# State-space layer: one batch's step-size exponentials moved ahead of the next decays in two of eight steps

## The chip, the cores and the metric

The kernel runs on one core of a Trainium2 chip. The metric is the device time of one execution in microseconds (us); the engines are TensorE (PE in the profile, with its weight loads as PEld), VectorE (DVE), ScalarE (ACT), GpSimd (POOL) and SyncE (SP), each with its own queue that it works through in order.

## The reference

A decoder of four blocks; each block has three layers (attention or a substitute, cross attention, a feed-forward part), and behind each the input is added and normalised. There are 4 sequences (batches) of 512 positions with 128 features. The change lies in the first layer of the second block, `L1_attn`, which is a state-space layer:

```python
xz = x @ W_in                                   # 128 -> 2 x 256
xi, z = jnp.split(xz, 2, axis=-1)
xc = silu(causal_conv4(xi, conv_w) + conv_b)    # 256 channels
dt, Bm, Cm = jnp.split(xc @ W_x, [8, 24], axis=-1)   # 8, 16 and 16 wide
delta = jax.nn.softplus(dt @ W_dt + b_dt)       # step sizes, 256 channels
A = -jnp.exp(A_log)                             # 256 x 16
dA = jnp.exp(delta[..., None] * A)              # decays
dBu = delta[..., None] * Bm[:, :, None, :] * xc[..., None]
h_t = dA_t * h_{t-1} + dBu_t                    # 16 states a channel
y_t = sum over states of h_t * C_t
y = y + xc * D
return y * silu(z) @ W_out
x = layernorm(x + that)
```

## The kernel before

All twelve layers run one after the other on the core, the tail of one interleaved with the start of the next. Every engine executes its instructions in the order in which the Python program emits them (`manual_schedule` for all five), so the order of the calls is the order of the queues; semaphores between engines follow from which instruction reads or writes which tile.

In `l1_attn` time runs along the free axis (512 positions) and the 256 channels are two halves `c` of 128 partitions. The 16 states are taken two at a time (`NQ = 2`), so a batch has `steps = 8` steps, and the loop over `g` runs through 4 x 8 = 32 steps plus one; `b` is the batch of a step and `j` its number in the batch. One step has these parts:

- `decays(g)`: four Exp activations on ScalarE (L2160), each of 511 elements, into `das[g % 2]`. They are issued one step ahead of their use.
- `spread(g, "B", c)` and `spread(g, "C", c)`: TensorE spreads one row of B or C over all partitions with a selecting weight (L2146 into two PSUM tiles `pb`, L2152 into a single PSUM buffer `pc`); ScalarE copies C to SBUF (`cs`, L2153). These too are one step ahead.
- `recurred(g)`: VectorE multiplies B with `du` (L2171) for both halves, then scans along time with the decays (L2174); GpSimd multiplies the states with C (L2178).
- `summed(g - 1, c)`: TensorE adds the states of the step before into PSUM (L2187), with an identity as weight.

Into this loop the next batch is prepared, by two agendas that run a piece at its step. `prepare(b + 1)` is called at `j == 1`. The agenda `early` then does at steps 1 to 6: the two halves of the convolution, `selected` (the product with `W_x`), `exponentials(0)`, `exponentials(1)`, and the gates. The agenda `late` does `logarithm(0)` at step 4 and `logarithm(1)` at step 5, and `third` (`ends`) at step 6 finishes the step sizes on GpSimd.

The softplus is formed as max(v, 0) + log(1 + exp(-|v|)), the logarithm by a polynomial in product form. `exponentials(c)` (L2097 to L2114) is one matmul into the PSUM tile `pdt` (L2100) and seven activations on ScalarE: Abs (L2105), Relu (L2106), two Exp (L2107, L2108) and three Squares (L2111). `logarithm(c)` (L2116 to L2122) is five VectorE instructions over `pdt`, the Squares `sq` and the exponential `ab`. `pdt`, the gates' `psz` and the products `px` and `pscv` share one PSUM buffer, and `sq` has one buffer for both halves, so `exponentials(1)` can start only when `logarithm(0)` is through. Before the loop, the first batch is prepared beside the previous layer, and the last batch has no successor to prepare, so `exponentials` runs in the loop in three batches.

In the kernel before, `early.run(g)` is called once a step, after the decays of the next step and after the first half of the sum, and ahead of the spreading:

Of the kernel before, what the change touches and what calls it, by code (L numbers as in the profile page):

```python
# [186 lines left out]
def decoder_kernel(ctx: ExitStack, tc: tile.TileContext, x, ctxT, mask1, mask3, packs, offsets, out, layers):  # L187
# [1844 lines left out]
    def l1_attn(w, cur, new, last, room):  # L2032
# [23 lines left out]
        early, late = Agenda(), Agenda()  # L2056
# [80 lines left out]
        def spread(g, kind, c):  # L2137

            b, j = divmod(g, steps)
            m = made[b]  # L2140
            if kind == "B":
                pb = psum2("pb")
                m["B", j, c] = pb
                for i in range(NQ):
                    n = j * NQ + i
                    nc.tensor.matmul(pb[:, i, :], lhsT=pick[:, n : n + 1].to_broadcast([P, P]), rhs=m["bc"], start=True, stop=True)  # L2146
                return
            if c == 0:
                m["C", j] = work[0].tile([P, NQ, S], F32, tag="cs", name="cs")
            pc = psum_v("pc", "a0")  # L2150
            n = NS + j * NQ + c
            nc.tensor.matmul(pc, lhsT=pick[:, n : n + 1].to_broadcast([P, P]), rhs=m["bc"], start=True, stop=True)  # L2152
            nc.scalar.copy(m["C", j][:, c, :], pc)  # L2153

        def decays(g):
            b, j = divmod(g, steps)
            for c in range(2):
                for i in range(NQ):
                    n = j * NQ + i
                    nc.scalar.activation(  # L2160
                        das[g % 2][:, c, i, 1:], made[b]["de"][:, c, 1:], AF.Exp, scale=nav[:, c, n : n + 1]
                    )

        def recurred(g):

            b, j = divmod(g, steps)
            m = made[b]
            m["h", j] = [work[0].tile([P, NQ, S], F32, tag=f"hh{c}", name=f"hh{c}") for c in range(2)]
            pbs = [m.pop(("B", j, c)) for c in range(2)]
            for c in range(2):  # L2170
                nc.vector.tensor_tensor(pbs[c], m["du"][:, c, None, :].to_broadcast([P, NQ, S]), pbs[c], ALU.mult)  # L2171
            for c in range(2):
                flat = m["h", j][c].rearrange("p n t -> p (n t)")
                nc.vector.tensor_tensor_scan(  # L2174
                    flat, das[g % 2][:, c].rearrange("p n t -> p (n t)"), pbs[c].rearrange("p n t -> p (n t)"),
                    0.0, ALU.mult, ALU.add,
                )
                nc.gpsimd.tensor_tensor(m["h", j][c], m["h", j][c], m["C", j], ALU.mult)  # L2178

        def summed(g, c):  # L2180
            b, j = divmod(g, steps)
            m = made[b]
            if j == 0 and c == 0:
                m["acc"] = [psum_v("acc", at) for at in "vy"]
            for i in range(NQ):
                n = j * NQ + i
                nc.tensor.matmul(  # L2187
                    m["acc"][c], lhsT=ident, rhs=m["h", j][c][:, i, :], start=(n == 0), stop=(n == NS - 1),
                    skip_group_check=True,
                )  # L2190

        def outputs(b):
            m = made.pop(b)
            yt = keep.tile([P, 2, S], F32, tag="yt", name="yt")
            for c in range(2):
                nc.vector.scalar_tensor_tensor(  # L2196
                    yt[:, c, :], m["xc"][:, c, :], w["dd"][:, c : c + 1], m["acc"][c], ALU.mult, ALU.add
                )
            nc.gpsimd.tensor_tensor(yt, yt, m["sz"], ALU.mult)
            ys = keep.tile([P, NT, D], F32, tag="ys", name="ys")  # L2200
            yps = []

            def projected():
                yp = psum_a("yps")
                yps.append(yp)
                for t in range(NT):
                    for c in range(2):
                        nc.tensor.matmul(
                            yp[:, t * P : (t + 1) * P], lhsT=yt[:, c, t * P : (t + 1) * P], rhs=wout[:, c, :],
                            start=(c == 0), stop=(c == 1),  # L2210
                        )

            def summed_up():
                nc.vector.tensor_tensor(
                    ys, yps[0].rearrange("p (t d) -> p t d", t=NT), state_x[:, b * NT : (b + 1) * NT, :], ALU.add
                )

            stats, norm, turn_over = finish_pieces(b, ys, new, last, split=True)
            return projected, summed_up, stats, norm, turn_over
# [29 lines left out]
        for g in range(total + 1):  # L2249
            b, j = divmod(g, steps)  # L2250
            if j == 1 and b + 1 < B:
                first, second, third = prepare(b + 1)
                early.add(g, first)
                late.add(g + 3, second)
            if j == 6 and b + 1 < B:
                third()
            if g < total:
                recurred(g)
            if g + 1 < total:
                decays(g + 1)  # L2260
            for c in range(2):
                if 0 <= g - 1 < total:
                    summed(g - 1, c)
                if c == 0:
                    early.run(g)
                if g + 1 < total:
                    spread(g + 1, "B", c)
                    spread(g + 1, "C", c)
            if j == 0 and b >= 1:
                late.run(g)  # L2270
                pieces = outputs(b - 1)
                if b < B:
                    early.add(g + 7, pieces[:1])
                    late.add(g + 7, [lambda two=pieces[1:3]: [f() for f in two]])
                    late.add(g + 8, [lambda end=pieces[3:]: [f() for f in end]])
            late.run(g)
            new["room"] = room_ahead if j % 2 and b == B - 1 else None
            yield PIECE
# [7 lines left out]

    run = dict(
        L0_attn=l0_attn, L0_xattn=l0_xattn, L0_ffn=l0_ffn, L1_attn=l1_attn, L1_xattn=l1_xattn, L1_ffn=l1_ffn,
        L2_attn=l2_attn, L2_xattn=l2_xattn, L2_ffn=l2_ffn, L3_attn=l3_attn, L3_xattn=l3_xattn, L3_ffn=l3_ffn,
    )  # L2290
# [156 lines left out]
```

## Time and profile before

| | us |
|---|---|
| median of 3 runs | 2677.82 (2677.05 to 2679.14) |
| profiled execution | 2676.14 |
| its span, first to last instruction | 2674.3 |
| state-space layer, first to last multiply-and-scan step | about 545 to 820 of the span |
| busy over the whole span: PE, DVE, ACT, POOL | 2413.6, 1708.0, 1244.2, 1056.5 |

One execution is profiled; times in the profile count from its first instruction. In a group's line the first part is line, engine, operation, and output<-inputs, then the shapes and how often; after the first bar busy time in us and the mean of one in ns; after the second the idle time of the engine just before these instructions, and what ended most of it. In a timeline a line has its start, its length, and in square brackets the idle time before it with what released it. A matmul in 32-bit floats shows as two records (two passes). In a table of stretches the columns are the length and the busy time of PE, PEld, DVE, ACT and POOL, each with its number of instructions, then TensorE's granted clock as a part of full speed, the DMA share and GB/s. In the waits the columns are who waited for whom, us in total, how often, and the longest.

### The profile page before, as it was taken

The numbers are of one execution on the slowest core, as the hardware profiler recorded it, in microseconds if no ns is written. First come the engines' busy times: TensorE is split into PE (matmuls) and PEld (weight loads), VectorE is DVE, ScalarE is ACT, GpSimd is POOL, SyncE is SP. The second block draws the span as 40 slices with busy tenths as digits, with TensorE's granted clock in tenths as the row PEclk, the third lists the DMA queues.
The fourth block names the chain that finished last, engine by engine and source line by source line (L and its number), as shares of the span: only waits on it lengthen the run. The fifth ranks groups of instructions, "written<-read, shape, count | busy, mean of one in ns | idle before, by whom it ended". The sixth has DMA issues, their size and how long they took to land.

```text
span 2674.3 us, 37907 instructions
## 1 busy us (share of the span) xinstructions
PE 2413.6 (90%) x14198; PEld 1171.3 (44%) x14218; DVE 1708.0 (64%) x3092; ACT 1244.2 (47%) x2517; POOL 1056.5 (40%) x1376
## 2 busy tenths in 40 slices
PE   5998889978877989999999999997988899899998
PEld 1333334433334444444444555554455333445665
DVE  6896951289997665555555555565855888564444
ACT  3775432377652434333233555453543678343221
POOL 2342520157675327555542444443345242320000
PEclk9998999989988999999999999998998899999999
DMA  5421310000002400000000000002102231310000
GB/s 154 120 80 58 102 36 0 0 0 0 0 16 76 149 7 1 0 1 1 0 1 1 15 1 13 13 6 80 51 1 60 67 99 41 129 45 5 13 11 14
DMA packets 76712, 97.98 MB, mean 37 GB/s; under 512 B 24048, under 2 KB 62704, under 8 KB 76528
## 3 DMA queue, kind: packets, MB, share of 16 engines
q1 hardware_dynamic: 75376, 93.72, 12.2%
q8 instruction: 112, 1.84, 0.3%
q10 hardware_dynamic: 1152, 1.84, 0.2%
q14 instruction: 72, 0.59, 0.1%
HBM read 63.92 MB, written 33.49 MB: 36 GB/s over the span
## 4 chain that ended last, share of the span: by engine, by line
PE 65%; DVE 14%; ACT 8%; POOL 5%; issue 4%; DMA 2%; SPq 1%; POOLq 0%; DVEq 0%; ACTq 0%
PE av L721 4%; PE psgu L1962 4%; PE psve L1312 4%; PE scc L1149 4%; PE avc L1222 3%; PE yT L1355 3%; PE ype L1978 3%; PE ptc L1209 3%; PE psh L1647 3%; ACT pr L1183 3%; PE sc L682 2%; DVE top L979 2%; PE avx L1007 2%; PE psqk L1494 2%; PE st L698 2%
## 5 line engine op out<-in xcount | busy, mean ns | idle before, releaser
L1193 POOL TENSOR_TENSOR pr<-pr,zs 128x1024 f32<-128x1024 f32 x192 | 237.4, 1254 | 236.2 <-DVE zs L1190 207.3
L686 DVE TENSOR_REDUCE top<-sc 128x2 f32<-128x1024 f32 x256 | 300.8, 1216 | 44.8 <-PE sc L682 42.1
L707 ACT ACTIVATE pT<-st 128x512 f32<-128x512 f32 x512 | 276.2, 597 | 88.6 <-PE st L698 85.3
L1183 ACT ACTIVATE pr<-scc,nm 128x256 f32<-128x256 f32 (+3 forms) x384 | 198.5, 527 | 177.7 <-DVE nm L1171 99.1
L979 DVE TENSOR_REDUCE top<-scx 128x4 f32<-128x616 f32 x256 | 192.1, 794 | 88.1 <-PE scx L966 76.9
L985 ACT ACTIVATE pTx<-stx 128x512 f32<-128x512 f32 x256 | 139.2, 596 | 204.3 <-PE scx L966 145.6
L2178 POOL TENSOR_TENSOR hh<-hh,cs 128x1024 f32<-128x1024 f32 x64 | 149.3, 2355 | 74.5 <-DVE hh L2174 50.8
L1171 DVE TENSOR_REDUCE nm<-scc 128x2 f32<-128x1024 f32 (+3 forms) x128 | 102.4, 821 | 118.5 <-PE scc L1156 118.5
L721 PE MATMUL av<-pT,vbuf 128*32 128x256 f32 x2048 | 162.8, 393 | 8.3 <-ACT avs L521 8.3
L504 POOL CAST nmP<-top 128x16 bf16<-128x16 f32 x96 | 25.7, 267 | 364.5 <-DVE top L979 202.8
L1317 DVE TENSOR_TENSOR vtmp<-psve,gm 128x1024 f32<-128x1024 f32 x64 | 78.3, 1224 | 132.8 <-PE psve L1312 132.7
L349 POOL TENSOR_TENSOR rsf<-mvf,eps 128x4 f32<-128x4 f32 x48 | 9.9, 206 | 377.8 <-DVE mvf L347 376.9
L1149 PE MATMUL scc<-k,q 64*128 64x512 f32 (+3 forms) x768 | 142.9, 470 | 7.4 <-DVE vtmp L1317 3.3
L2174 DVE TENSOR_TENSOR_SCAN hh<-da,pb 128x1024 f32<-128x1024 f32 x64 | 142.6, 2270 | 0.0
L1209 PE MATMUL ptc<-ident,pr 128*128 128x128 f32 x960 | 136.8, 280 | 6.2 <-POOL pr L1193 4.2
L1312 PE MATMUL psve<-w_L_ffn,xT 128*128 128x512 f32 x256 | 125.3, 614 | 17.4 <-ACT pr L1183 11.9
L682 PE MATMUL sc<-kP,qP 64*128 64x512 bf16 x512 | 106.7, 415 | 34.3 <-DMA qP<-far_q 16.1
L1322 POOL TENSOR_TENSOR vtmp<-vtmp 128x512 f32<-128x512 f32 x60 | 76.3, 1272 | 153.1 <-DVE vtmp L1317 132.8
L2187 PE MATMUL acc<-hh,ident 128*128 128x512 f32 x256 | 131.8, 641 | 3.1 <-DVE yt L2196 2.0
L1222 PE MATMUL avc<-pT,v 128*64 128x512 f32 (+3 forms) x768 | 131.4, 449 | 0.5 <-DVE pT L1545 0.5
L1209 PEld LDWEIGHTS ptc<-ident,pr 128*128 128x128 f32 x960 | 103.5, 141 | 46.0 <-issue 20.5
L1355 PE MATMUL yT<-gT,w_L_ffn 128*128 128x512 f32 x256 | 123.2, 604 | 0.0
(423 smaller groups left out, 5103.4 us busy)
## 6 DMA issues: line engine op xcount, KB each, us to landing
qP<-far_q SPq DMA_DIRECT2D x24, 768.0 KB, 6.4
w_L_ffn<-in_L_ffn SPq DMA_DIRECT2D x24, 512.0 KB, 6.1
far_q<-part SPq DMA_DIRECT2D x44, 192.0 KB, 2.8
qP<-far_q SPq DMA_DIRECT2D x24, 256.0 KB, 4.3
far_q<-part SPq DMA_DIRECT2D x44, 128.0 KB, 2.4
kP<-far_k SPq DMA_DIRECT2D x7, 768.0 KB, 5.1
kP<-far_kc SPq DMA_DIRECT2D x16, 231.0 KB, 4.8
w_L_attn<-in_L_attn SPq DMA_DIRECT2D x6, 512.0 KB, 6.6
```

The source lines that it names most:

```text
L682: nc.tensor.matmul(sc[:, r, :], lhsT=m["q"][rows, 2 * j + gp, qt * P : (qt + 1) * P], rhs=m["k"][rows, 2 * j + gp, :], start=True, stop=True,)
L686: return lambda: nc.vector.tensor_reduce(top[:, qt, 2 * gp : 2 * gp + 2], sc, AX.X, ALU.max, negate=True)
L707: nc.scalar.activation(pT, st, AF.Exp)
L721: nc.tensor.matmul(m["av"][32 * g : 32 * g + 32, part], lhsT=m["v"][:, kt, 4 * j + g, :], rhs=weights_of[s, g][:, part], start=(kt == 0 an ...
L979: nc.vector.tensor_reduce(ops.maxima(a)[:, 2 * qp : 2 * qp + 2, 2 * gp : 2 * gp + 2].rearrange("p i r -> p r i"), sc, AX.X, ALU.max, negat ...
L1149: nc.tensor.matmul(sc[:, r, at : at + n], lhsT=q[rows, qt * P : n], rhs=k[rows, :n], start=(i == 0), stop=not self.by_pe, skip_group_check ...
L1183: nc.scalar.activation(pr[:, r, at:to], sc[:, r, at:to], AF.Exp, bias=nm[:, i, r : r + 1], scale=1.0 if self.by_pe else -1.0, accum_out=zs ...
L1193: nc.gpsimd.tensor_tensor(pr[:, :, at : at + n], pr[:, :, at : at + n], zs[:, i, :, None].to_broadcast([P, 2, n]), ALU.mult)
L1209: nc.tensor.transpose(pt[:, r, to : to + P], self.pr[u, p][:, r, lo : lo + P], ident)
L1222: nc.tensor.matmul(av[64 * r : 64 * r + 64, kt * P :], lhsT=v[:, kt, 64 * r : 64 * r + 64], rhs=self.pT[u, part][:, r, at : at + n], start ...
L1312: nc.tensor.matmul(ps[:, r, :], lhsT=src[:, t * P : (t + 1) * P], rhs=w["ve"][:, h * 512 : (h + 1) * 512], start=True, stop=True,)
L1355: nc.tensor.matmul(yTs[b], lhsT=oe[:, c, e, :], rhs=gT[:, i, :], start=(c == 0 and e == 0), stop=(c == NC - 1 and e == NE - 1),)
```

## The change

In steps 4 and 5 of every batch, `early.run(g)` is called once more, and earlier: after `recurred(g)` and before `decays(g + 1)`. A run takes the pieces of its step out of the agenda, so that the later call of the same step finds nothing. `exponentials(0)` and `exponentials(1)` are thus emitted ahead of the four decays of the next step and ahead of the first half of the sum; their matmul stands earlier on TensorE and their seven activations earlier on ScalarE.

```diff
             if g < total:
                 recurred(g)
+            if j in (4, 5):
+
+                early.run(g)
             if g + 1 < total:
                 decays(g + 1)
             for c in range(2):
                 if 0 <= g - 1 < total:
                     summed(g - 1, c)
                 if c == 0:
                     early.run(g)
```

## The prediction

> **What bounds the kernel now.** I read the page first (busy shares, costliest groups), then the busy time by stretch for the state-space layer, then the waits of that layer, and last the timelines of the single engines around steps 4 to 7 of the second batch, where the moved work sits.
>
> The groups of 545 to 825 us, by line:
>
> ```profile
> L2178 POOL TENSOR_TENSOR hh<-hh,cs 128x1024 f32<-128x1024 f32 x64 | 149.3, 2355 | 74.5 <-DVE hh L2174 50.8 <-ACT da L2160 23.3
> L2174 DVE TENSOR_TENSOR_SCAN hh<-da,pb 128x1024 f32<-128x1024 f32 x64 | 142.6, 2270 | 0.0
> L2160 ACT ACTIVATE da<-de,na 128x511 f32<-128x511 f32 x128 | 81.7, 712 | 0.1
> L2171 DVE TENSOR_TENSOR pb<-du,pb 128x1024 f32<-128x1024 f32 x64 | 75.7, 1219 | 9.8 <-PE pb L2146 8.7 <-PE psz L2080 0.6 <-POOL du L2126 0.5
> ```
>
> The same stretch whole:
>
> ```profile
> 545.00:825.00 280.00, 222.64 (x588) 94.30 (x595) 257.91 (x217) 179.57 (x279) 195.07 (x111) 0.91 0.02 5
> ```
>
> Two of the waits from 540 to 830 us:
>
> ```profile
> DVE pb L2171 <- PE pb L2146: 8.7, 8, 2.7
> ...
> DVE pdt L2120 <- ACT sq L2111: 7.2, 3, 2.4
> ```
>
> VectorE is busy for 257.9 of 280 us; ScalarE (179.6) is not the bound. The scans never wait for the decays (idle 0.0), so ScalarE's order is not late for them. But VectorE has two waits that repeat by batch: 2.4 us for the Squares, and up to 2.7 for the B rows from TensorE. These are the places to watch. ScalarE, second batch:
>
> ```profile
> 648.13 0.59 ACT L2153 COPY cs<-pc 128x512 f32<-128x512 f32 x1 [0.46 <-PE pc L2152]
> 648.61 2.56 ACT L2160 ACTIVATE da<-de,na 128x511 f32<-128x511 f32 x4
> 651.07 0.67 ACT L2105 ACTIVATE ab<-pdt,w_L_attn 128x512 f32<-128x512 f32 x1
> ...
> 653.52 1.83 ACT L2111 ACTIVATE sq<-pdt,shifts 128x512 f32<-128x512 f32 x3
> 655.23 0.59 ACT L2153 COPY cs<-pc 128x512 f32<-128x512 f32 x1
> ...
> 668.43 0.59 ACT L2153 COPY cs<-pc 128x512 f32<-128x512 f32 x1 [2.51 <-PE pc L2152]
> ```
>
> VectorE, the same time:
>
> ```profile
> 648.49 4.45 DVE L2174 TENSOR_TENSOR_SCAN hh<-da,pb 128x1024 f32<-128x1024 f32 x2
> 655.38 2.15 DVE L2120 SCALAR_TENSOR_TENSOR pdt<-sq,pdt 128x512 f32<-128x512 f32 x3 [2.43 <-ACT sq L2111]
> ...
> 679.08 1.23 DVE L2171 TENSOR_TENSOR pb<-du,pb 128x1024 f32<-128x1024 f32 x1 [1.79 <-PE pb L2146]
> ```
>
> TensorE:
>
> ```profile
> 647.72 0.38 PE L2152 MATMUL pc<-bc,pick 128*128 128x512 bf16 x1 [0.54 <-ACT cs L2153]
> 647.93 1.88 PE L2187 MATMUL acc<-hh,ident 128*128 128x512 f32 x4
> 649.74 1.12 PE L2100 MATMUL pdt<-rest,w_L_attn 8*128 8x512 f32 x2
> ...
> 659.04 2.07 PE L2100 MATMUL pdt<-rest,w_L_attn 8*128 8x512 f32 x2
> 663.50 1.03 PE L2146 MATMUL pb<-bc,pick 128*128 128x512 bf16 x2 [2.39 <-DVE hh L2174]
> ...
> 673.43 1.74 PE L2080 MATMUL psz<-xT,w_L_attn 128*128 128x512 f32 x2 [2.46 <-ACT sz L2081]
> ```
>
> In front of the seven activations stand the decays, 2.46 us of ScalarE that no scan needs before 661; behind them VectorE stands still for 2.43.
>
> **The change part by part.** Nothing is added or removed. In steps 4 and 5 of three batches (six places; the first batch's own preparation and the last batch have none), one matmul and seven activations (Abs, Relu, two Exp, three Squares) are emitted before the four decays instead of behind them. On TensorE the matmul also passes one half of the sum over states (L2187, 1.72 us). No DMA, POOL or SP instruction moves, and VectorE's order stays.
>
> *Step 4, exponentials(0).* The pdt matmul takes the slot behind the pc matmul: 647.93, plus the 0.09 by which it started late behind its predecessor (649.74 against 647.93 + 1.72), so 648.02; with 1.12 it ends at 649.14, and Abs starts at 649.18 instead of 651.07: 1.89 earlier. ScalarE idles for some 0.46 us ahead of it (the copy ends at 648.72). The seven pitch 4.16 (651.07 to 655.23), so logarithm(0) starts at 653.49. The scans end at 652.95, hence the wait is 0.54 instead of 2.43. The same reckoning gives 1.89 in the first batch (Abs at 581.94 for 583.83) and 1.90 in the third. Sum: **5.7 us**. Costs: the decays end at about 656 and their scan starts at 653.49 + 3.52 + 2.26 = 659.3, a cover of 3.5; the sum over states moves to 649.1 to 650.8, and the B rows behind it start at 650.83 anyway, since they wait for a scan. Both cost nothing. If the first cover were gone, each us of delay would be a us on VectorE.
>
> *Step 5, exponentials(1).* Here a wait gets a queue behind it. The pdt matmul needs the one PSUM buffer that logarithm(0) still uses, 3.66 us from that one's start (655.38 to 659.04). I count from this start, L. Behind the matmul now stand half a sum and the next B and C rows on TensorE; behind its Abs stand the decays of step 6 and both C copies on ScalarE. From L, at full clock: Abs 4.82 (the matmul's 1.16, first batch), decays 4.82 + 4.16 = 8.98, first C copy 11.44, second C copy 11.44 + 0.59 + 0.05 + 0.41 = 12.49. Before, that copy came at 14.25, 13.05 and 13.97, because the sum in front of it ran at about half clock: TensorE had stood still just before, for 3.3 us in the first and third batch and 2.4 in the second. logarithm(1) needs its Squares by 3.52 + 6.64 = 10.16 and has them at 9.1. The decays of step 6 end at 11.4; their scan comes at 15.9. POOL needs the copied C only at 18.2. So this wait alone costs VectorE nothing.
>
> *Step 7, what the copy leads to.* From that second copy runs a chain: decays, a table load of 1.28, the first gate, the second gate's matmul, half a sum, the B row that VectorE waits for. It took 8.95 us in the first batch (602.38 to 611.33), and 10.65 in the second and third (668.43 to 679.08), where the second gate's matmul and what follows ran at half clock. VectorE wants that row at L + 3.52 + 6.64 + 3.52 + 6.64 + 1.14 = 21.46. Before, scan 7 was late by 1.76, 2.27 and 3.19, in all 7.2. After, the row comes at 12.49 + 8.95 = 21.44, no wait, if TensorE keeps its clock; a slow pdt (2.07 for 1.12) adds 0.95, a slow gate stretch 1.70.
>
> Does it keep it? The new gap before the second pdt is 2.6 us (B row done at 653.8, C row at 656.4), then one short matmul and 0.3 more; the gate gap stays at 2.4. The row: after the 2.46 us gap at 671 the psz matmul took 1.74 instead of 1.12, and so in two batches of three the stretch was slow. [...] By the row, gaps of 2.4 us drop it two times in three: 3 x 2/3 x (1.70 + 0.95) = 5.3 of waiting left, a gain of 7.2 - 5.3 = **1.9**. I take the row. With everything slow, 7.9 is left and 0.7 lost.
>
> Sum: 5.7 + 1.9 = 7.6 us. The profiled execution took 2676.14 (span 2674.3), which gives 2668.5; it lay 1.7 below the median of 2677.82, and against that it is 2670.2. VectorE has no wait over 0.5 us between 772 and 823, so what is won reaches the layer's end.
>
> An unseen cost would be the activations' tables: Copy, Abs, Relu, Exp and Square in a new order. In all eight groups of L2105 to L2111 the trace has one table load, where a Silu had gone before; the decays' Exp table is in at both places. I take zero.
>
> **The rivals.**
>
> *Step 7 takes it back.* VectorE's 5.7 us are only worth something if the B rows of step 7 come as much earlier. For it: they end a chain through ScalarE and TensorE with its own waits. Against: the chain starts at logarithm(0)'s end, which moves too. With all three batches slow at both places it is 5.7 - 0.7 = 5.0 gained; with a further us a batch, 2. Some 2673 to 2676, no measurable difference.
>
> [...]
>
> *Slower: TensorE stays at half clock from the second pdt on.* One mechanism: the matmul waiting for logarithm(0) leaves TensorE idle, and all of what queues behind it is slow. Slow pdt, then 3.41 for half a sum (first batch), so the B rows of step 6 at L + 9.0 instead of 8.1; C, 3.41 again, then B and C: the second copy at about 15.2, the row of step 7 at 15.2 + 10.65 = 25.9, a wait of 4.4 a batch. That is 13.2 for 7.2: with the 5.7, 0.3 lost, 2678.1. It decides from a second copy later than L + 15.1; if the slow clock also reached a convolution (3.42 us of matmuls in front of the next B rows), up to 3 x 3.4 more, 2688. Against: from the pdt on, TensorE has work for over 4 us, and the slow stretches of the trace ended after 3.5 to 6 us of such work.
>
> That the order is not what the edit says I rule out: engine order follows emission, and the agenda empties a step that has been run, so its later call does nothing.
>
> **How the numbers follow.** About 0.2% (5.4 us) is what a measurement of this kernel can tell from no change. My case, both gains with a clock now fast, now slow (5.0 to 10.5), gets 0.63, of which some 0.05 lies under 5.4; the whole gain 0.12; taken back 0.16; slower or something unseen 0.09. That makes 0.70 faster, 0.21 within, 0.09 slower. The range reaches from nearly the whole gain (12.3) to one mostly taken back (1.8): 2665.5 to 2676.0.
>
> **What would show it.** In the changed profile: VectorE's wait for the Squares (7.2 us, 3 times) at about 1.5; Abs of step 4 straight behind the C copy with some 0.46 idle; decays of step 5 behind the Squares; the scans still at idle 0.0; VectorE's wait for the B rows at 4 to 8 us in all; the second pdt directly after logarithm(0), with half a sum behind it. I am wrong if the scans wait for decays, if Abs of step 4 does not move 1.9 earlier, or if the B rows of step 7 hold VectorE for over 10 us.

## The result, and the profile after

The changed kernel takes 2667.72 us in the median of 10 runs (2663.92 to 2672.96), the kernel before 2675.62 in 10 (2671.02 to 2681.37): a ratio of 0.997, 95% interval 0.9959 to 0.998, or 7.9 us less. In a later comparison it was 2668.66 against 2674.9, a ratio of 0.9973 (0.9965 to 0.9982). The forecast was 2670.2, a gain of 7.6 against the median then known; the measured gain lies within its range of 1.8 to 12.3. The time itself was forecast 2.5 us too high, mostly because the three runs of the kernel before that were known then had a median of 2677.82, 2.2 above that of the ten.

The profiled execution has a span of 2663.8 us, 10.5 less than before. Of this, 2.7 us lie ahead of the first step that the change touches: the scans of step 3 of the first batch start at 572.06 instead of 574.76. Nothing was altered ahead of it, and the thirteen profiled executions of this study in which that is so reach that scan anywhere from 569.66 to 577.34, so this part is scatter and no gain. From that scan to the last one the time falls from 240.61 to 232.95 us, by 7.66. Two waits make up 7.62 of it: that for the first Squares is 5.61 us shorter in all, and the first scans of step 7 are 2.01 less late (the table below has both).

VectorE's groups from 545 to 825 us, after:

```profile
L2174 DVE TENSOR_TENSOR_SCAN hh<-da,pb 128x1024 f32<-128x1024 f32 x64 | 142.6, 2269 | 0.0
...
L2171 DVE TENSOR_TENSOR pb<-du,pb 128x1024 f32<-128x1024 f32 x64 | 75.6, 1218 | 8.0 <-PE pb L2146 7.5 <-POOL du L2126 0.5
```

Two of its waits from 530 to 830 us (the prediction's lines of before were from 540 on):

```profile
DVE pb L2171 <- PE pb L2146: 7.5, 7, 2.4
...
DVE pdt L2120 <- ACT sq L2111: 2.0, 4, 0.6
```

The last line counts one wait in the first batch's own preparation (0.5 us), outside the loop; the three in the loop make 1.5, where there were 7.2. The wait for B rows shrank little by this line, but it also holds waits of other steps. The scans still never wait for decays. ScalarE, second batch:

```profile
643.61 0.59 ACT L2153 COPY cs<-pc 128x512 f32<-128x512 f32 x1 [0.46 <-PE pc L2152]
644.66 0.69 ACT L2105 ACTIVATE ab<-pdt,w_L_attn 128x512 f32<-128x512 f32 x1 [0.47 <-PE pdt L2100]
...
648.84 2.55 ACT L2160 ACTIVATE da<-de,na 128x511 f32<-128x511 f32 x4
...
654.51 0.69 ACT L2105 ACTIVATE ab<-pdt,w_L_attn 128x512 f32<-128x512 f32 x1 [1.59 <-PE pdt L2100]
...
662.17 0.59 ACT L2153 COPY cs<-pc 128x512 f32<-128x512 f32 x1 [0.46 <-PE pc L2152]
```

VectorE beside it:

```profile
648.99 2.16 DVE L2120 SCALAR_TENSOR_TENSOR pdt<-sq,pdt 128x512 f32<-128x512 f32 x3 [0.56 <-ACT sq L2111]
...
671.13 1.23 DVE L2171 TENSOR_TENSOR pb<-du,pb 128x1024 f32<-128x1024 f32 x1 [0.62 <-PE pb L2146]
```

And TensorE:

```profile
651.92 0.38 PE L2152 MATMUL pc<-bc,pick 128*128 128x512 bf16 x1 [2.58 <-ACT cs L2153]
652.66 1.81 PE L2100 MATMUL pdt<-rest,w_L_attn 8*128 8x512 f32 x2 [0.36 <-DVE ln L2122]
654.40 3.78 PE L2187 MATMUL acc<-hh,ident 128*128 128x512 f32 x4
```

Abs of step 4 follows the C copy with 0.47 us of idleness, the decays stand behind the Squares, and VectorE waits 0.56 instead of 2.43. The second pdt starts right after logarithm(0) but takes 1.81 us instead of 1.12, and the half sum behind it 3.78 instead of 1.88: the granted clock there is 0.50, from 652.96 to 659.79, and 1.00 from 649.00 to 652.96 and from 659.79 to 670.50. The second C copy of step 6 comes 13.18 us after logarithm(0)'s start (662.17 less 648.99).

### The profile page after: what moved, and what is told of

Its sections match the earlier page's. It is cut to its first block, busy times and chain, and to the rows that moved or that the text cites. A ratio compares the mean times of both kernels' runs of the same rounds, so it can differ in the third digit from the quotient of the medians.

```text
span 2663.8 us, 37907 instructions
## 1 busy us (share of the span) xinstructions
PE 2410.4 (90%) x14198; PEld 1170.1 (44%) x14218; DVE 1708.4 (64%) x3092; ACT 1244.1 (47%) x2517; POOL 1056.0 (40%) x1376
## 3 DMA queue, kind: packets, MB, share of 16 engines
q8 instruction: 112, 1.84, 0.3%
q10 hardware_dynamic: 1152, 1.84, 0.2%
## 4 chain that ended last, share of the span: by engine, by line
PE 64%; DVE 15%; ACT 8%; POOL 6%; issue 4%; DMA 3%; SPq 1%; POOLq 0%; DVEq 0%; ACTq 0%
PE psgu L1962 4%; PE psve L1312 4%; PE av L721 4%; PE scc L1149 4%; PE yT L1355 3%; PE avc L1222 3%; PE ype L1978 3%; PE ptc L1209 3%; PE psh L1647 3%; ACT pr L1183 3%; DVE top L979 2%; PE sc L682 2%; PE psqk L1494 2%; PE avx L1007 2%; DVE top L686 2%
```

## The experiments

Three numbers can be read from the starts of VectorE's instructions in each profiled execution, summed over the three batches: the wait for the first Squares, the wait for the second Squares, and by how much scan 7 (the first scan of step 7) starts later than the 6.62 us after scan 6 that its work needs. The table has them, with the measured medians of all kernels; the experiments are told below it. The three numbers are of one execution each, the medians of 5 to 20. "Before" was measured anew in each of the later groups: 2676.13 with the first four, 2676.6 with the next four, 2674.9 with the two after them, 2675.85 with the last.

| kernel | first Squares | second Squares | scan 7 late | median us | ratio to before (95%) |
|---|---|---|---|---|---|
| before | 7.16 | 0 | 7.28 | 2675.62 | |
| changed | 1.55 | 0 | 5.27 | 2667.72 | 0.9970 (0.9959 to 0.9980) |
| step 4 alone | 1.55 | 3.94 | 4.63 | 2671.52 | 0.9981 (0.9973 to 0.9988) |
| step 5 alone | 7.16 | 0 | 6.34 | 2672.64 | 0.9986 (0.9978 to 0.9994) |
| matmul alone | 7.16 | 0 | 0.12 | 2670.07 | 0.9976 (0.9968 to 0.9985) |
| activations alone | 6.69 | 8.20 | 5.18 | 2678.96 | 1.0010 (0.9999 to 1.0021) |
| mixed | 1.55 | 1.02 | 3.38 | 2665.01 | 0.9956 (0.9944 to 0.9969) |
| changed, gates split | 1.55 | 0 | 4.54 | 2666.95 | 0.9965 (0.9952 to 0.9977) |
| mixed, gates split | 1.55 | 1.02 | 3.95 | 2667.01 | 0.9959 (0.9946 to 0.9973) |
| changed, filler | 1.55 | 0 | 5.19 | 2665.46 | 0.9963 (0.9950 to 0.9975) |
| mixed, split, sums early in step 6 | 1.55 | 1.23 | 0.31 | 2666.98 | 0.9966 (0.9952 to 0.9980) |
| the same, sums early in all steps | 3.18 | 1.03 | 0.32 | 2681.93 | 1.0023 (1.0014 to 1.0031) |
| mixed, sums early in step 6 | 1.52 | 1.02 | 0 | 2661.75 | 0.9946 (0.9932 to 0.9959) |

**Each step alone.** Step 4 alone:

```diff
-            if j in (4, 5):
+            if j == 4:
                 early.run(g)
```

> Only exponentials(0), in step 4, stands ahead of the decays; step 5 is as it was before. My theory (ScalarE's place in the queue is worth 1.9 us a batch at step 4): VectorE's wait for the first Squares is about 0.5 a batch, as in the changed kernel, against 2.4. In step 5 the decays now come first again, so the second Squares may be 0.4 us late a batch, but the C copies of step 6 come up to 1 us earlier than in the changed kernel; step 7's waits between 1 and 5 us in all. Gain against the kernel before: 6 to 10 us, about 8. Rival (both moves are needed): under 5 us. Rival (TensorE's clock did it): the wait for the Squares stays near 2.4.

Step 5 alone has `j == 5` in its place.

> Only exponentials(1), in step 5, stands ahead of the decays. My theory: VectorE's wait for the first Squares stays at 2.3 to 2.4 us a batch; the second C copy of step 6 comes 12.5 to 13.4 us from the start of logarithm(0); scan 7 is late by 3 to 6 us in all instead of 7.2. Gain 1 to 4, about 2 us. Rival (step 5 carries the gain): 5 us or more. Rival (the matmul that waits at the head of TensorE's queue costs): slower than before.

Step 4 alone gains 4.6 us in the medians. The wait for the first Squares is as short as in the changed kernel, so the first part of the theory holds. The gain is less than the 6 to 10 us forecast, and the rival that both moves are needed (under 5 us) was right: I had put the second Squares at 0.4 us late a batch, and they were 0.34, 1.84 and 1.76. VectorE and TensorE of this kernel, second batch:

```profile
663.38 2.15 DVE L2120 SCALAR_TENSOR_TENSOR pdt<-sq,pdt 128x512 f32<-128x512 f32 x3 [1.84 <-ACT sq L2111]
```

```profile
654.43 3.13 PE L2187 MATMUL acc<-hh,ident 128*128 128x512 f32 x4
657.49 1.52 PE L2100 MATMUL pdt<-rest,w_L_attn 8*128 8x512 f32 x2
```

With logarithm(0) earlier, the half sum is no longer done by the time that the pdt may start; it takes 3.13 us, against 1.88 in the kernel before at 651.49, and the pdt comes 6.2 us after logarithm(0)'s start (651.29) instead of 3.7. So the move of step 5 has a use that I had not counted: it keeps what step 4 has won. Alone it is worth little: in the trace scan 7 is late by 6.34 (forecast 3 to 6) instead of 7.28, 0.9 us; the medians show 3.5 (interval 1.6 to 5.9). That it carries the whole gain is out, since the first Squares wait 7.16 us as before; and that it costs is out by the interval.

**Which engine's order.** The matmul alone (`early.run(g)` after `decays(g + 1)`, still ahead of the sum), and the activations alone (the half sum emitted first):

```diff
             if g + 1 < total:
                 decays(g + 1)
+            if j in (4, 5):
+                early.run(g)
```

> In steps 4 and 5 only the matmul stands earlier on TensorE, ahead of the half sum; the seven activations stand behind the decays as before. My theory (ScalarE's order is what counts in step 4): Abs of step 4 stays at 1.9 us later than in the changed kernel and the wait for the Squares at 2.3 to 2.4 a batch; only step 7 gains, 2 to 6 us. Rival (TensorE's order is what counts): the wait for the Squares falls to 0.5 a batch and the gain is the whole 7 to 8 us.

```diff
             if j in (4, 5):
+                summed(g - 1, 0)
                 early.run(g)
...
-                if 0 <= g - 1 < total:
+                if 0 <= g - 1 < total and not (c == 0 and j in (4, 5)):
                     summed(g - 1, c)
```

> In steps 4 and 5 only the seven activations stand ahead of the decays; the matmul stays behind the half sum on TensorE. My theory (ScalarE stands idle until the matmul is through, so both have to move): Abs of step 4 at most 0.2 us earlier than before, the wait for the Squares 2.1 to 2.3 a batch, TensorE's 3.3 us gap before the B rows of step 6 and its half clock stay as before; gain between -2 and 2 us, about 0.5. Rival (ScalarE's order alone does it): 5 us or more.

With the matmul alone the first Squares wait exactly as before, and yet 6.1 us are gained in the medians; in the trace the wait that goes is that of step 7 (0.12 us left of 7.28):

```profile
DVE pdt L2120 <- ACT sq L2111: 7.2, 3, 2.4
DVE pb L2171 <- PE pb L2146: 4.1, 5, 1.5
```

So step 4's gain is not to be had without ScalarE's order, and step 7's is had by TensorE's order: there the activations may as well stand behind the decays. That as much as 7.2 us goes at step 7 is in part luck, since no gate stretch (the second gate's matmul and the matmuls up to the next B row) was slow in this execution; that matmul took 1.12 us in the third batch. The activations alone lose 2.8 us in the medians (not clear of zero; the profiled execution lay 3.6 above its median). I had expected between 2 us lost and 2 gained; step 4's wait falls by 0.16 a batch as reckoned, but at step 5 the C copy stands behind everything, TensorE idles for 4.35 us, and the sum and the pdt behind it take 3.62 and 2.07 us, where the kernel before has 1.88 and 1.12 at a granted clock of 1.00 (602.17 and 649.74):

```profile
660.86 0.58 PE L2152 MATMUL pc<-bc,pick 128*128 128x512 bf16 x1 [4.35 <-ACT cs L2153]
661.24 3.62 PE L2187 MATMUL acc<-hh,ident 128*128 128x512 f32 x4
664.78 2.07 PE L2100 MATMUL pdt<-rest,w_L_attn 8*128 8x512 f32 x2
```

The second Squares are then late by 2.11, 3.04 and 3.05 us. Matmul and activations have to move together where the activations go ahead of the decays.

**Mixed**: step 4 as in the change, step 5 with the matmul alone.

```diff
+            if j == 4:
+                early.run(g)
             if g + 1 < total:
                 decays(g + 1)
+            if j == 5:
+                early.run(g)
```

> Step 4 as in the changed kernel (matmul and activations ahead of the decays); in step 5 only the matmul ahead of the half sum, the activations behind the decays. My theory (two separate gains: ScalarE's order in step 4, TensorE's order in step 5): wait for the first Squares about 0.5 a batch, none for the second, scan 7 late by 0 to 2 us in all; gain against the kernel before 9 to 13 us, against the changed kernel 2 to 5 less time. Rival (the two gains are one and the same slack): no better than the changed kernel, 7 to 8 us. Rival (with logarithm(0) earlier, the second Squares come late as in the kernel with step 4 alone, 1.8 a batch): 5 to 8 us.

It gains 11.6 us in the medians; its interval (8.3 to 15.0) overlaps that of the changed kernel, and its profiled execution was the fastest of its five. Both gains are there at once, at a price of 0.34 us a batch for the second Squares (scan 7 is late by 3.38, not 0 to 2: two of the three batches had a slow stretch).

**What holds step 7.** The second gate behind the C copies of step 6 (a third entry in the agenda of the logarithms), in the changed kernel and in the mixed one (the preparation of the first batch, ahead of the loop, keeps its order by a line that is left out here):

```diff
-                    lambda: exponentials(1), lambda: (gates(0), gates(1)),
+                    lambda: exponentials(1), lambda: gates(0),
...
-                [lambda: logarithm(0), lambda: logarithm(1)],
+                [lambda: logarithm(0), lambda: logarithm(1), lambda: gates(1)],
```

> The changed kernel, but the second gate (matmul and Silu) stands behind the last C copy of step 6 instead of between the first gate and the B rows. My theory (step 7's wait is the chain C copy, decays, table load, first gate, second gate's matmul, B row): VectorE's wait for B rows at step 7 falls from 5.2 in all to 0 to 3, what is left coming from half-clock sums; gain against the kernel before 10 to 13 us. Rival (step 7 waits for something else on ScalarE or TensorE): scan 7 stays late by about 5, gain 7 to 8.

> Both: step 4 whole, step 5 the matmul alone, the second gate behind the last C copy. My theory: first Squares 0.5 a batch, scan 7 late by 0 to 2 us in all; gain 11 to 13.5 us, the fastest of all. Rival (nothing is left once one of the two is done): the same as the better of the two alone.

Both missed: scan 7 stays late by 4.54 and 3.95, and the gains are 9.7 and 9.6 us. The gate is out of the chain, but TensorE then idles in front of the first B row instead (3.0 to 3.3 us), and in five of the six batches the sum between the two B rows is slow (3.62 us in the rows here, 1.88 at a granted clock of 1.00 in the kernel before); in the sixth scan 7 is not late. TensorE of the mixed one, second batch:

```profile
670.32 1.03 PE L2146 MATMUL pb<-bc,pick 128*128 128x512 bf16 x2 [3.08 <-DVE hh L2174]
671.15 0.63 PE L2152 MATMUL pc<-bc,pick 128*128 128x512 bf16 x1
671.58 3.62 PE L2187 MATMUL acc<-hh,ident 128*128 128x512 f32 x4
```

**Is it the idleness?** The filler repeats the second B rows of step 4 six times into the same place, while TensorE would stand idle:

```diff
                     spread(g + 1, "B", c)
+                    if c == 1 and j == 4 and b + 1 < B:
+                        pb = made[b]["B", j + 1, 1]
+                        for _ in range(6):
+                            for i in range(NQ):
+                                n = (j + 1) * NQ + i
+                                nc.tensor.matmul(
+                                    pb[:, i, :], lhsT=pick[:, n : n + 1].to_broadcast([P, P]), rhs=made[b]["bc"],
+                                    start=True, stop=True,
+                                )
                     spread(g + 1, "C", c)
```

> The changed kernel with extra work: in step 4 of three batches the two matmuls of the second B rows are done six times more, into the same place, in the 2.6 us in which TensorE stands idle ahead of the second pdt. Theory of the clock (an idle stretch of 2.6 us is enough to halve it): the second pdt takes 1.12 in all three batches instead of 1.2, 1.8 and 2.1, Abs of step 5 comes 4.8 to 5.0 us from the start of logarithm(0), the second C copy of step 6 at 12.5; the gate stretch is free to be slow or fast; gain against the changed kernel 0 to 3 us, in spite of the added 36 matmul pairs. Rival (the slow matmuls have nothing to do with idleness): the same durations as in the changed kernel, and no gain.

```profile
650.61 2.75 PE L2276 MATMUL pb<-bc,pick 128*128 128x512 bf16 x12
653.36 0.38 PE L2152 MATMUL pc<-bc,pick 128*128 128x512 bf16 x1
654.10 1.12 PE L2100 MATMUL pdt<-rest,w_L_attn 8*128 8x512 f32 x2 [0.36 <-DVE ln L2122]
655.15 1.98 PE L2187 MATMUL acc<-hh,ident 128*128 128x512 f32 x4
...
667.92 1.82 PE L2080 MATMUL psz<-xT,w_L_attn 128*128 128x512 f32 x2 [2.46 <-ACT sz L2081]
```

The pdt takes 1.12 us in all three batches, the sum behind it 1.98 in the second instead of 3.78, and the second C copy comes at 12.49 in all three. In the profile of the changed kernel a spell with a granted clock of 0.50 begins within 1.3 us of the second pdt's start in each batch: at 588.15 (the pdt at 587.23), 652.96 (652.66) and 721.27 (722.48). So in this kernel TensorE's idleness is the cause of the slow pdt. The gap of 2.46 us in front of the second gate is untouched, and there the stretch is slow in all three, so scan 7 is late by 1.73 in each: the time won at the pdt is lost again, and from step 3 on the trace takes 232.91 us, as the changed kernel (232.95). The medians do not tell the two apart. The table of stretches, second batch from logarithm(0) on; first the changed kernel, then the filler:

```profile
649.00:670.50 21.50, 16.04 (x34) 5.91 (x34) 21.23 (x19) 16.69 (x27) 16.24 (x8) 0.84 0.00 0
```

```profile
650.40:671.90 21.50, 16.27 (x44) 6.23 (x43) 21.20 (x19) 16.74 (x27) 16.23 (x8) 0.92 0.00 0
```

The 0.84 is the one spell at 0.50 from 652.96 to 659.79, over the pdt and the sum, with 1.00 in the rest. For the 0.92 I estimate 2 x 0.08 x 21.5 = 3.4 us at 0.50 from this row, with 1.00 in the rest; the slow matmul of the filler's row is that of the second gate (1.82 us at 667.92), which in the changed kernel took 1.12 at a granted clock of 1.00 (667.17).

**Sums early.** In step 6 alone, and in all steps, both halves of the sum are emitted ahead of the B rows, on top of the mixed kernel with the gates split; the second kernel has `ahead = True`:

```diff
+            ahead = j == 6
             for c in range(2):
-                if 0 <= g - 1 < total:
+                if 0 <= g - 1 < total and not (c == 1 and ahead):
                     summed(g - 1, c)
+                    if ahead:
+                        summed(g - 1, 1)
```

> The kernel with step 4 whole, step 5's matmul alone and the second gate behind the C copies, and in step 6 of every batch both halves of the sum stand ahead of the B rows, so that TensorE has work until 1 us before the first B row and no slow sum between the two B rows. Theory (what is left of step 7's wait is one half-clock sum between the B rows, after an idle stretch of 3 us): scan 7 late by 0 to 0.3 a batch, gain against the kernel before 12 to 14 us. Rival (the wait has another cause): scan 7 still late by about 1.3 a batch, gain about 9.

> The same with both halves of the sum ahead of the B rows in every step. Theory: as with step 6 alone, 12 to 14 us, and B rows that follow one another directly may also take away part of the 1.5 us that scan 2 and the 1.3 us that scan 0 to 1 are late in a batch (convolution in front of the B rows): up to 5 us more. Rival (the second half of the states is not there yet and holds TensorE): a part of the gain is lost, 5 to 12 us.

> The changed kernel as it is, beside the two others: 6 to 10 us less than the kernel before.

With step 6 alone scan 7 is late by 0.1 a batch, as the theory had it, but the gain stays at 7.9 us instead of 12 to 14: the second gate now stands in front of the next step's sum and of the output product `yps`, and step 8 (step 0 of the next batch) becomes later by 1.2, 1.1 and 1.4 us. In the second batch VectorE waits for that product:

```profile
682.70 0.69 DVE L2214 TENSOR_TENSOR ys<-yps,x 128x512 f32<-128x512 f32 x1 [0.96 <-PE yps L2208]
```

The wait moved one step on. In all steps the kernel is slower than before by 7 us, where theory and rival both had a gain. Its one profiled execution, the shortest of its runs, shows only where it begins: scans 2 to 4 become later, the first Squares too (1.06 instead of 0.5 us a batch), and step 8 by 0.4, 2.6 and 2.5 us; and the whole from step 3 of the first batch on takes 241.29 us, 0.7 more than before. The rest of the 7 us stays open. The changed kernel beside them gained 6.2.

**The last version** keeps both gates in their old place and has the early sums in step 6, on the mixed kernel.

> Step 4 whole, step 5's matmul alone, both gates at their old place, and in step 6 both halves of the sum ahead of the first gate. Theory: the sum leaves the chain from the C copy to the B row of step 7 (8.95 at full clock, 10.65 with a half-clock stretch, becomes about 7.2), and fills the stretch in which TensorE stood idle between the two gates; no matmul is pushed into the next step. So scan 7 late by 0 to 0.3 a batch, and step 8 as before (0, 2.3, 2.3); gain against the kernel before 11 to 13 us. Rival (whatever is moved only moves the wait one step on): step 8 late by 1 us more a batch, gain 8 to 9.

```profile
DVE pb L2171 <- PE pb L2146: 2.6, 4, 1.1
...
DVE pdt L2120 <- ACT sq L2111: 2.5, 6, 0.6
```

TensorE in step 6 of its second batch:

```profile
662.90 3.64 PE L2187 MATMUL acc<-hh,ident 128*128 128x512 f32 x8
666.38 1.02 PE L2080 MATMUL psz<-xT,w_L_attn 128*128 128x512 f32 x2
668.10 1.13 PE L2080 MATMUL psz<-xT,w_L_attn 128*128 128x512 f32 x2 [0.70 <-ACT sz L2081]
670.32 0.39 PE L2146 MATMUL pb<-bc,pick 128*128 128x512 bf16 x1 [1.10 <-DVE hh L2174]
```

Scan 7 is not late at all, step 8 is as before, and the median is 2661.75 against 2675.85: 14.1 us, a ratio of 0.9946, somewhat more than the 11 to 13 forecast. The sum stands ahead of the first gate and takes up time in which TensorE stood idle between the two, so that this gap falls from 2.46 to 0.70 us, and the B rows wait only for their own scan. It has the lowest median of the study; its interval (0.9932 to 0.9959) just touches that of the changed kernel (0.9959 to 0.9980) and overlaps that of the mixed one.

## Why the prediction was right, point by point

- **Step 4.** Predicted: 1.89 us a batch, waits of 0.41 to 0.54 left. Measured: 0.43, 0.56, 0.56 instead of 2.30, 2.43, 2.43, that is 5.61 in all for 5.7. Step 4 alone and the mixed kernel show the same waits, so it is this move that makes them; the activations alone show that the matmul has to come along.
- **Step 5.** Abs came at 4.94, 5.52 and 5.78 us, the second C copy at 12.60, 13.18 and 13.44; the forecast was 12.49 at full clock and 13.44 with a slow pdt. That nothing on VectorE waits for the step was right. Not counted was that leaving it out would have cost 3.9 us: the step's worth was put too low, though the sum, which had both moves in it, does not change by this.
- **Step 7.** Predicted: 5.3 us of lateness left, from stretches slow two times in three. Measured 5.27. The chain from the C copy to the B row took 10.66, 8.96 and 10.66, the two lengths that the trace of before had. The agreement is closer than the argument deserved: how often a stretch is slow differs from one execution to the next, and the second profile of the changed kernel has 5.85, with all three gate stretches slow. The two in three was read from three batches, and in the third of them the gate's matmul itself took 1.12; what was slow there was the sum behind it (3.28).
- **The end of the layer.** That no later wait would take the gain was so in the profile compared here, and not in every execution: in the second profile of the changed kernel the scans of step 2 of the last batch are 1.56 us late, which in the profiles of before and after they are not.
- **The clock.** The row, a slow stretch behind a gap of 2.46, held: behind that gap the granted clock of the changed kernel fell to 0.50 in the first and the third batch (at 601.75 and 738.33) and stayed at 1.00 in the second, and at the new gap of 2.50 to 2.58 us it fell in all three (588.15, 652.96 and 721.27). The whole gain, to which the prediction gave 0.12 and which sets the upper end of its range, needs both gaps to be harmless. No run of this kernel shows that: 5.27 of the 7.28 us at step 7 were left.
- **The cases.** What is left waits at step 7 as forecast, so neither the full gain nor the taking back came about. The half clock of the slower case came in part: the pdt was slow in two batches of three (1.81 and 2.07 us; 1.23 in the other) and the half sum behind it in all three, but the next sum took 2.15 us in the second batch and 1.88 in the others, so the C copy was not late by more than 1 us.

## What to carry to other kernels

When VectorE waits for a chain that ScalarE starts late, look for work ahead of it in the queue that nobody needs yet, and move the chain's matmul along with its activations. Then follow the freed time to the next wait: here the change won 7.9 us of the 14.1 that the last version reached, and the rest was held by TensorE, whose gaps of 2.46 to 2.58 us between matmuls came with a granted clock of 0.50 in five cases of six in the changed kernel's profile. Moving a matmul out of a chain did not shorten the wait while the gap moved along with it. Work that is due anyway can fill such a gap: the sum did, in the last version.

## What the runs showed of the hardware

A gap of about 2.5 us was often, and not always, followed by slow matmuls: behind the gate gap of 2.46 us the stretch was slow in two batches of three before and after, in three of three in the second profile of the changed kernel and with the filler, and in none with the matmul alone, where the gaps were 2.24 to 2.46. In the kernel before, the granted clock is 0.50 from 673.81 to 677.22 and from 748.96 to 752.37, behind the gaps of the second and the third batch; behind that of the first it is 1.00 from 607.37 to 611.30. The second gate's matmul there, first and second batch:

```profile
607.37 1.12 PE L2080 MATMUL psz<-xT,w_L_attn 128*128 128x512 f32 x2 [2.46 <-ACT sz L2081]
```

```profile
673.43 1.74 PE L2080 MATMUL psz<-xT,w_L_attn 128*128 128x512 f32 x2 [2.46 <-ACT sz L2081]
```

The gap is 2.46 us in both, and one was followed by a spell and the other was not. So the length of the gap alone does not decide; what does is not shown here.

Executions of one unaltered kernel spread over 10 us (2671.02 to 2681.37), and in the profiled pair 2.7 us of difference arose ahead of any altered instruction, 1.1 of it in a step with a slower half sum (3.62 us for 2.96) and convolution (4.04 for 3.59); so with a change of this size a single pair of profiles is to be read by its waits, and not by its spans.
